# Two key steps' values in one run, and what moves with it, in an attention and expert block on one Trainium2 core

## The chip, the core and the metric

The kernel runs on one core of a Trainium2 chip. The core has a matrix engine (PE, with the loading of its weights shown apart as PEld), a vector engine (DVE), a scalar engine (ACT), a general engine (POOL) and an engine that only issues transfers (SP). Each works through its own queue in order. Matrix products land in PSUM banks, which ACT and DVE read; everything else lies in SBUF. The metric is the device time of one execution in microseconds (us), lower is better.

## The reference, cut to what matters

```
x = layernorm(x + attention(x))        # x: 2 x 1024 x 512, 16 heads of 32
x = layernorm(x + moe(x))              # 8 experts, 256 slots each, and a shared expert

attention: q, k, v = projections of x with low-rank updates
           scores = q k^T / sqrt(32);  attn = softmax(scores);  out = attn v
           out projection with a low-rank update
```

Only the attention's inner part, from scores to `attn v`, is touched by the change. It is full float32 in its result.

## The kernel before, in words

The work is cut into 16 **units** of 128 partitions' worth of heads: two batches, four groups of four heads, two halves of 512 queries. A unit has eight **key steps**, one for each 128 keys, so the main loop (`for t in range(NS)`) has 128 steps, `u, k = t // 8, t % 8`. All five engines' orders are written out by hand there: what the loop issues is what each queue holds, in that order.

A step does this:

- `st_step` (line 620): four PE matmuls, one for each head, scores with keys on the partitions. After each, ACT takes the exponential into one half of a tile `pts[t, 0]` or `pts[t, 1]` (line 629). There are 14 such tiles (`PTB`), seven steps' worth. The four places after the four heads are the step's quarters, and `between[q]` lists what else is issued in quarter q.
- `s1_step` (line 189): one matmul with queries on the partitions, and a DVE maximum over its 512 keys (line 197). Four are done in each step, for a step that comes 12 steps (`LEAD`) later; 32 make the row maxima of one unit. `finish_max` transposes these on PE (line 207) and sends them as two rows into the tile of queries, so that `st_step` subtracts them. It is called from the first `s1_step` of the next unit, at quarter `MPP`.
- `av_step` (line 639): four matmuls of values with the exponentials, each 32 columns wide and in its own column tile of PE, all into one bank `avs[u]`. It is issued for the step before, in the second quarter.
- `adds`: the exponentials of a unit are merged so that their row sums need few matmuls. The table `ADDS` says which: `b` takes a tile as the sum, `d` adds a tile into the next one with a DMA (line 656), `p` and `v` add on POOL or DVE (line 659).
- `finish` (line 672): the row sums, as products with ones, of the merged tile and of the tiles that `direct` names. For most units the sums then go through DRAM to another shape (`sd`, `r16`); `invert` takes the reciprocal there and sends it back (`rd`, then four broadcasts `rb`). From unit `RDIR` on, DVE takes the reciprocal of the whole 128 x 512 tile (line 682).
- `normalize` (lines 711 to 718): DVE multiplies the values with the inverse, ACT copies the high part, DVE subtracts for the low part. For two units DVE does the copy too.
- In steps 65 to 80 four to eight matmuls of the first batch's output projection (`oproj`, line 744) stand at a step's end.

PSUM has three banks for `st_step` (shared with the row sums and the transposed maxima, `one`), three for `s1_step` (`s1p`), two for the values (`avp`).

Loads are issued by SP: keys of a group (two units) into one of two tiles, in halves of 512 keys, the first half at k 6 of the unit before (`K_AT`) and the second at k 0; queries of a unit two units ahead at k 0.

Before the loop come the projections, after it the second half of the output projection, the router and the experts.

Of the kernel before, what the change touches and what calls it, by code (L numbers as in the profile page):

```python
# [13 lines left out]
ALU = mybir.AluOpType  # L14
# [5 lines left out]
B, L, D = 2, 1024, 512  # L20
NU = 16
T = B * L
NH, HD = 16, 32
NG = 4
# [8 lines left out]
LEAD = 12  # L33
LATE, OP_ONE = (0,), 1
NS = NU * 8
# [14 lines left out]
}  # L50
MAN3 = {mybir.EngineType.PE}
MAN4 = MAN2 - MAN3
DIRECT = (7,)
NO_DIR = (NU - 2,)
FIN, FINQ = 4, 1
REC = 5
NRM = 0
K_AT = 6
XTB = 5


ADDS = {
    None: {0: "bb0", 2: "dd1", 3: "pp3", 4: "pp4", 5: "pp2", 6: "pp5", 7: "pp6"},
    NU - 3: {0: "bb0", 2: "dd1", 3: "pp3", 4: "pp4", 5: "pp2", 7: "dd6 pp5"},
    NU - 2: {1: "bb1 dd0", 3: "dd2", 5: "dd4", 6: "vv3", 7: "vv6 vv7 vv5"},
    NU - 1: {1: "bb1 dd0", 3: "dd2", 4: "vv4", 5: "vv5", 6: "vv3 vv6"},
}
OPROJ_AT = (65, 67, 69, 71, 73, 75, 77, 79)
RES_AT = tuple(8 * i + (2 if i % 2 else 6) for i in range(8)) + (70, 74, 86, 90, 100, 102, 106, 110)
RES_ADDS = tuple(t + 3 for t in RES_AT[:14]) + (119, 120)  # L70
RB = 2
# [1 line left out]
AHEAD = 5  # L73
W2_END = {2: (0, 1, 2), 3: (3, 4), 4: (5,)}
W2_AT = {2: (0, 1), 3: (2, 3), 4: (4,), 5: (5,)}
MPJ, MPP = 0, 2
RDIR = NU - 3
FINE, NRME = 2, {NU - 2: 6, NU - 1: 4}
OPROJ1 = 0
NRM_DVE = (NU - 3, NU - 2)  # L80
ROOT_LAG, NORM_LAG = 1, 4
# [17 lines left out]
def kernel(  # L99
# [3 lines left out]
    pe, act, dve, pool, sp = nc.tensor, nc.scalar, nc.vector, nc.gpsimd, nc.sync  # L103

    def f(ap):
        return ap.bitcast(F32)
# [42 lines left out]
    def load_k(g, cs=slice(0, 1024), hs=slice(0, 4)):  # L149
        kt = Ks[g % 2]  # L150
        for blk, hl in ((0, 0), (1, 1), (2, 0)):
            sp.dma_start(
                out=f(kt[32 * blk : 32 * blk + 32, hs, cs]),
                in_=qk_d[1, g // NG, g % NG, hl].rearrange("(h p) t -> p h t", p=32)[:, hs, cs],
            )
# [23 lines left out]
    mts, pts, avs, accs, vts = {}, {}, {}, {}, {}  # L179


    def s1_step(s, part):
        u, j = s // 8, s % 8
        g = u // 2
        if j == 0 and part == 0:
            mts[u] = mp_.tile([P, 16, 2], F32, name=f"mt{u}", tag="mt", bufs=2)
        h, qt, kh = j // 2, 2 * (j % 2) + part // 2, part % 2
        s1 = s1p.tile([P, 512], F32, name=f"s1_{u}_{h}_{qt}_{kh}", tag="s1")
        pe.matmul(  # L189
            s1,  # L190
            Qs[u % 3][0:96, h, qt * P : qt * P + P],
            Ks[g % 2][0:96, h, kh * 512 : kh * 512 + 512],
            start=True,
            stop=True,
        )
        c = h * 4 + qt
        dve.tensor_reduce(mts[u][:, c, kh : kh + 1], s1, AX.X, ALU.max)  # L197
        if j == 7 and part == 3:
            mx = mp_.tile([P, 16], F32, name=f"mx{u}", tag="mx", bufs=2)
            dve.tensor_reduce(mx, mts[u], AX.X, ALU.max)  # L200
            mts[u] = mx
        if j == MPJ and part == MPP and u:
            finish_max(u - 1)

    def finish_max(u):
        mp = one.tile([P, 512], F32, name=f"mp{u}", tag="one")
        pe.transpose(mp[0:16, 0:P], mts[u], ident)
        mh = mp_.tile([16, P], F32R, name=f"mh{u}", tag="mh", bufs=2)
        ml = mp_.tile([16, P], F32R, name=f"ml{u}", tag="ml", bufs=2)
        act.copy(mh, mp[0:16, 0:P])  # L210
        dve.tensor_tensor(ml, mp[0:16, 0:P], f(mh), ALU.subtract)
        for i, m_ in enumerate((mh, ml)):
            sp.dma_start(
                out=f(Qs[u % 3][96 + i : 97 + i, :, :]).rearrange(
                    "o h (q t) -> o (h q) t", t=P
                ),
                in_=f(m_),
            )
# [382 lines left out]
    with ph2, tc.manual_schedule(engines={mybir.EngineType.PE}):  # L601
# [31 lines left out]
        def av_step(t):  # L633
            u, kc = t // 8, t % 8
            g = u // 2
            if kc == 0:
                avs[u] = avp.tile([P, 512], F32, name=f"av{u}", tag="av")
            for h in range(4):
                pe.matmul(  # L639
                    avs[u][32 * h : 32 * h + 32, :],  # L640
                    vts[g][:, kc, 32 * h : 32 * h + 32],
                    pts[t, h // 2][:, h % 2, :],
                    start=kc == 0,
                    stop=kc == 7,
                    skip_group_check=True,
                )

        def adds(t):
            u, kc = t // 8, t % 8
            for op in ADDS.get(u, ADDS[None]).get(kc, "").split():  # L650
                i = u * 8 + int(op[2])
                for pr in range(2):
                    if op[pr] == "b":
                        accs[u, pr] = pts[i, pr]
                    elif op[pr] == "d":
                        pool.dma_start(out=pts[i + 1, pr], in_=pts[i, pr], accum_op=ALU.add)  # L656
                    else:
                        eng = dve if op[pr] == "v" else pool
                        eng.tensor_tensor(accs[u, pr], accs[u, pr], pts[i, pr], ALU.add)  # L659

        def direct(u):
            return () if u in NO_DIR else DIRECT

        fin = {}

# [40 lines left out]
        def normalize(u, parts=(0, 1, 2)):  # L706
            g, qb = u // 2, u % 2
            cs = slice(qb * 512, qb * 512 + 512)
            hi, lo = at_h[:, g % NG, cs], at_l[:, g % NG, cs]
            if 0 in parts:  # L710
                dve.tensor_tensor(avs[u], avs[u], fin[u], ALU.mult)
            if 1 in parts:
                if u in NRM_DVE:
                    dve.tensor_copy(hi, avs[u])
                else:
                    act.copy(hi, avs[u])
            if 2 in parts:
                dve.tensor_tensor(lo, avs[u], f(hi), ALU.subtract)
# [42 lines left out]
        op10 = oproj(1, 0, 3)  # L761
        steps = ExitStack()
        steps.enter_context(tc.manual_schedule(engines=MAN2))
        for t in range(NS):
            u, k = t // 8, t % 8
            if k == 0:

                if u % 2 == 0 and 2 <= u and u // 2 + 1 < B * NG:
                    for hs in (slice(0, 2), slice(2, 4)):
                        load_k(u // 2 + 1, slice(512, 1024), hs)  # L770
                        load_q(u + 2, hs)
                elif u >= 1 and u + 2 < NU:
                    load_q(u + 2)
                if u % 2 and NG <= u // 2 + 1 < B * NG:
                    load_v(u // 2 + 1)

            if k == K_AT and u % 2 and u // 2 + 2 < B * NG:
                load_k(u // 2 + 2, slice(0, 512))
            if t in RES_AT:
                load_res(RES_AT.index(t))  # L780
            between = [[], [], [], []]
            if t + LEAD < NS:
                for q in range(4):
                    between[q].append(lambda q=q: s1_step(t + LEAD, q))
            elif t + LEAD == NS:
                between[0].append(lambda: finish_max(NU - 1))
            if t:
                between[1].append(lambda: av_step(t - 1))
                between[1].append(lambda: adds(t - 1))
                if u and k == (FINE if u == NU - 1 else FIN):  # L790
                    between[1 if u == NU - 1 else FINQ].append(lambda: finish(u - 1))
            if u:
                if k == NRM and 1 < u < NU - 1:
                    for q in range(3):
                        between[q].append(lambda q=q: normalize(u - 2, (q,)))
                if k == NRME.get(u):
                    for q in range(3):
                        between[(0, 3, 3)[q]].append(lambda q=q: normalize(u - 1, (q,)))
            if t in RES_ADDS:
                between[3].append(lambda: add_res(RES_ADDS.index(t)))  # L800
            st_step(t, between)
            if k == REC and 1 <= u <= RDIR:
                invert(u - 1)
            if t in OPROJ_AT:
                op0 = oproj(0, OPROJ_AT.index(t), OPER)
            if OPROJ_AT[0] <= t:
                next(op0, None)
            if t + 1 in OPROJ_AT[1:]:
                run(op0)
            for _, fn in [x for x in later if x[0] == 0]:  # L810
                fn()
            later[:] = [(n - 1, fn) for n, fn in later if n]
            if t - NS >= OPROJ1:
                next(op10, None)
        av_step(NS - 1)
        adds(NS - 1)
        finish(NU - 1)
        normalize(NU - 1, (0,))
# [302 lines left out]
    for st in range(NB):  # L1121
# [18 lines left out]
        if st == NB - 3:  # L1140
            reads_xd(
                sp.dma_start(
                    out=meta, in_=xd_d[:, D : D + 2].rearrange("(j p) c -> p j c", p=P)
# [132 lines left out]
```

## Time and profile before

| | |
|---|---|
| median of 3 runs | 1062.13 us (1060.24 to 1062.37) |
| the profiled execution | 1048.99 us, its span 1047.3 us |
| granted PE clock | 0.996 |
| main loop | about 155 to 606 us |
| experts and the rest after it | about 607 to 1047 us |

The profile is of one execution. A line of its timeline says when an instruction or a row of the same instructions started, how long it took, the engine, the line of the program, the operation, what it wrote and read, how many there are, and in brackets how long the engine was idle before it and what it had waited for. The windows view gives, for each stretch, each engine's busy time and number of instructions.

| stretch, us | PE busy | DVE | ACT | POOL |
|---|---|---|---|---|
| 205.00 to 372.00 | 166.86 | 135.78 | 110.92 | 165.73 |
| 372.00 to 462.00 | 89.49 | 67.51 | 50.19 | 71.75 |
| 462.00 to 560.00 | 98.00 | 80.16 | 67.22 | 96.59 |
| 560.00 to 607.00 | 44.84 | 37.33 | 31.83 | 13.48 |

The first and third are units with all their parts, the second holds most of the output projection's matmuls, the last has the steps for which no `s1_step` is left.

### The profile page before, as it was taken

How to read it: one execution, taken by the hardware profiler on the slowest of the kernel's cores; microseconds unless marked ns; L12 is line 12 of the kernel's file. 1: busy time of each engine (PE TensorE's matmuls, PEld its weight loads, DVE VectorE, ACT ScalarE, POOL GpSimd, SP SyncE). 2: the span in 40 equal slices, each digit the busy share in tenths (PEclk: the TensorE clock that was granted, in tenths of full speed). 3: DMA queues.
4: the chain of work that ended last, by engine and by line, in shares of the span. 5: the costliest groups of instructions: out<-in, count | busy, mean ns of one | idle time of the engine just before them, and what ended most of it. 6: DMA issues, size and time to landing. Idle time of an engine off the chain costs nothing. (4 is left out here: it accounts for less than half of the span.)

```text
span 1047.3 us, 16557 instructions
## 1 busy us (share of the span) xinstructions
PE 1026.7 (98%) x5994; PEld 741.5 (71%) x5994; DVE 687.7 (66%) x1192; ACT 527.2 (50%) x1023; POOL 573.2 (55%) x406
## 2 busy tenths in 40 slices
PE   8999999999999999999999999999999999999995
PEld 6888774444444455545444379899999999999994
DVE  7732788788888878788887974233522567777752
ACT  5422216666666656566666645223222456555552
POOL 4000005999999987879996255000140046676674
PEclk9999999999999999999999999999999999999998
DMA  9876863364646563444657632000182556777721
GB/s 294 278 231 210 250 204 81 87 141 103 141 94 148 120 140 83 100 92 120 150 121 161 142 106 67 22 21 21 41 253 81 156 183 219 253 246 248 256 81 60
DMA packets 86025, 151.93 MB, mean 145 GB/s; under 512 B 15492, under 2 KB 24196, under 8 KB 85944
## 3 DMA queue, kind: packets, MB, share of 16 engines
q1 hardware_dynamic: 76344, 117.31, 37.7%
q0 software_dynamic: 9600, 33.58, 13.6%
q8 instruction: 47, 0.77, 0.3%
q14 instruction: 34, 0.28, 0.1%
HBM read 95.83 MB, written 33.78 MB: 124 GB/s over the span
## 5 line engine op out<-in xcount | busy, mean ns | idle before, releaser
L197 DVE TENSOR_REDUCE mt<-s 128x1 f32<-128x512 f32 x512 | 323.9, 681 | 78.7 <-PE s L189 78.3
L659 POOL TENSOR_TENSOR pt<-pt,pt 128x1024 f32<-128x1024 f32 x138 | 336.0, 2917 | 0.1
L629 ACT ACTIVATE pt<-st 128x512 f32<-128x512 f32 x512 | 269.1, 601 | 131.5 <-PE st L620 114.2
L620 PE MATMUL st<-qs,ks 98*128 98x512 f32 x512 | 213.1, 427 | 1.1 <-DVE x1a L347 0.7
L189 PE MATMUL s<-ks,qs 96*128 96x512 f32 x512 | 200.2, 398 | 1.1 <-DVE mt L197 1.1
L620 PEld LDWEIGHTS st<-qs,ks 98*128 98x128 f32 x512 | 95.6, 188 | 133.0 <-issue 93.1
L656 POOL DMA_DIRECT2D pt<-pt x40 | 36.9, 1101 | 187.2 <-PE st L620 164.2
L890 PE MATMUL h<-xthe,w13s 128*128 128x256 f32 x704 | 129.9, 284 | 0.0
L878 POOL TENSOR_TENSOR w2s<-w2r,w2s 128x512 fp32r<-128x512 f32 x42 | 65.9, 1590 | 93.1 <-ACT w2s L877 92.2
L189 PEld LDWEIGHTS s<-ks,qs 96*128 96x128 f32 x512 | 97.0, 189 | 20.5 <-DVE mt L197 5.8
L890 PEld LDWEIGHTS h<-xthe,w13s 128*128 128x128 f32 x704 | 110.6, 191 | 0.3
L890 PE MATMUL h<-xtle,w13s 128*128 128x256 f32 x352 | 100.2, 285 | 0.1
L639 PE MATMUL av<-pt,vt 128*32 128x512 f32 x512 | 75.3, 605 | 0.0
L1038 POOL DMA_INDIRECT xd_d<-x1a,slot_i x8 | 7.9, 985 | 110.5 <-DVE slot_i L1035 108.4
L639 PE MATMUL av<-pt,x1b 128*32 128x512 f32 x512 | 68.2, 605 | 0.0
L890 PEld LDWEIGHTS h<-xtle,w13s 128*128 128x128 f32 x352 | 67.4, 191 | 1.0 <-DVE xtle L468 0.3
L934 PE MATMUL y<-w2s,hs 128*128 128x512 f32 x260 | 60.9, 390 | 0.0
L934 PEld LDWEIGHTS y<-w2s,hs 128*128 128x128 f32 x260 | 48.2, 188 | 10.2 <-DVE hs L916 0.5
L331 ACT ACTIVATE oh<-o,bqk_sb 128x512 fp32r<-128x512 f32 x32 | 22.0, 690 | 57.1 <-PE o L316 52.7
L901 ACT ACTIVATE sl<-h 128x256 f32<-128x256 f32 x40 | 15.5, 386 | 60.5 <-PE h L890 59.2
L316 PE MATMUL o<-xh,wh 128*128 128x512 f32 x116 | 45.3, 391 | 0.3 <-DVE ol L332 0.3
L316 PE MATMUL o<-xl,wh 128*128 128x512 f32 x116 | 45.3, 390 | 0.1
(830 smaller groups left out, 1831.9 us busy)
## 6 DMA issues: line engine op xcount, KB each, us to landing
pt<-pt POOLq DMA_DIRECT2D x40, 512.0 KB, 6.4
x1a<-in_w_dram SPq DMA_DIRECT2D x24, 512.0 KB, 5.6
w2r<-in_w_dram SPq DMA_DIRECT2D x42, 256.0 KB, 2.9
qkd<-oh SPq DMA_DIRECT2D x32, 256.0 KB, 2.3
qkd<-ol SPq DMA_DIRECT2D x32, 256.0 KB, 2.5
x1b<-in_w_dram SPq DMA_DIRECT2D x16, 512.0 KB, 7.0
qs<-qkd SPq DMA_DIRECT2D x30, 256.0 KB, 4.4
ks<-qkd SPq DMA_DIRECT2D x18, 256.0 KB, 4.6
```

Source lines behind the costliest of these rows:

```text
L189: pe.matmul(s1, Qs[u % 3][0:96, h, qt * P : qt * P + P], Ks[g % 2][0:96, h, kh * 512 : kh * 512 + 512], start=True, stop=True,)
L197: dve.tensor_reduce(mts[u][:, c, kh : kh + 1], s1, AX.X, ALU.max)
L316: pe.matmul(o, lhs, rhs, start=k + i == 0, stop=k + i == KC + 1)
L331: act.activation(oh, o, AF.Identity, bias=bias)
L620: pe.matmul(sb, Ks[g % 2][:, h, kc * P : kc * P + P], Qs[u % 3][:, h, :], start=True, stop=True,)
L629: act.activation(pts[t, h // 2][:, h % 2, :], sb, AF.Exp, scale=SCALE)
L639: pe.matmul(avs[u][32 * h : 32 * h + 32, :], vts[g][:, kc, 32 * h : 32 * h + 32], pts[t, h // 2][:, h % 2, :], start=kc == 0, stop=kc == 7 ...
L656: pool.dma_start(out=pts[i + 1, pr], in_=pts[i, pr], accum_op=ALU.add)
L659: eng.tensor_tensor(accs[u, pr], accs[u, pr], pts[i, pr], ALU.add)
L878: pool.tensor_tensor(hl[:, 1, :], raw, f(hl[:, 0, :]), ALU.subtract)
L890: pe.matmul(hp[:, j * 256 : j * 256 + 256], lhs, rhs[:, k, :], start=n == 0, stop=n == 11,)
L934: pe.matmul(o, lhs, rhs, start=n == 0, stop=n == 16)
```

## The change

- `av_step` is issued for two steps at once, at even steps, in the fourth quarter (`AVQ`).
- The 32 `s1_step` calls of eight steps are no longer one for each quarter. A table `S_AT` gives for each step and quarter how many stand ahead of the values and how many behind them. Their order among themselves is the same. `MPP` goes from 2 to 1.
- `ADDS`: most units now add tile 2 into tile 1 and tile 3 into tile 0 with DMAs, and tiles 4, 5, 6 and 0 into tile 1 on POOL. The DMA's target is now given by the table. Before, one DMA added tile 1 into tile 2, and POOL added tiles 3, 4, 2, 5 and 6 into tile 0.
- `DIRECT`: the last unit takes the row sums of tiles 6 and 7 straight. DVE's adds for it fall from eight to six.
- `FIN`, `REC` and `NRM` give unit offset, step and quarter of the row sums, the inverse and normalize. For most units: row sums at step 4 of the next unit, quarter 1, as before; the inverse at step 6 instead of 5; normalize at step 1 of the unit after, instead of step 0.
- `RDIR` goes up by one: unit 13 takes the way through DRAM.
- Keys are loaded whole at k 0, in two halves of the heads; the load at k 6 is gone.
- The output projection's steps go from 65 to 79 to 66 to 80.

```
-DIRECT = (7,)
-NO_DIR = (NU - 2,)
-FIN, FINQ = 4, 1
-REC = 5
-NRM = 0
-K_AT = 6
+DIRECT = {None: (7,), NU - 2: (), NU - 1: (6, 7)}
+AVQ = 3
+FIN = {None: (1, 4, 1), NU - 3: (1, 3, 1), NU - 2: (1, 2, 3)}
+REC = {None: (1, 6, 3), NU - 3: (1, 5, 3)}
+NRM = {
+    None: ((2, 1, 0), (2, 1, 2), (2, 1, 2)),
+    NU - 3: ((2, 0, 1), (2, 0, 1), (2, 0, 1)),
+    NU - 2: ((1, 4, 1), (1, 4, 1), (1, 4, 1)),
+}
+S_AT = (
+    ((0, 0), (0, 1), (1, 0), (1, 0)), ((0, 0), (0, 1), (1, 1), (0, 0)),
+    ((0, 2), (1, 0), (0, 0), (0, 2)), ((0, 0), (0, 1), (0, 2), (0, 0)),
+    ((0, 1), (1, 2), (0, 1), (1, 1)), ((1, 0), (0, 0), (2, 0), (1, 0)),
+    ((0, 0), (1, 0), (0, 1), (1, 0)), ((0, 1), (1, 0), (0, 0), (2, 0)),
+)
 ADDS = {
-    None: {0: "bb0", 2: "dd1", 3: "pp3", 4: "pp4", 5: "pp2", 6: "pp5", 7: "pp6"},
-    NU - 3: {0: "bb0", 2: "dd1", 3: "pp3", 4: "pp4", 5: "pp2", 7: "dd6 pp5"},
-    NU - 2: {1: "bb1 dd0", 3: "dd2", 5: "dd4", 6: "vv3", 7: "vv6 vv7 vv5"},
-    NU - 1: {1: "bb1 dd0", 3: "dd2", 4: "vv4", 5: "vv5", 6: "vv3 vv6"},
+    None: {1: "bb1 dd21", 2: "dd30", 3: "pp4", 4: "pp5", 5: "pp6", 6: "pp0"},
+    NU - 2: {1: "bb1 dd01", 3: "dd23", 5: "dd45 vv6 vv3", 6: "vv7", 7: "vv5"},
+    NU - 1: {1: "bb1 dd01", 3: "dd23 vv4", 4: "vv5", 6: "vv3"},
 }
-OPROJ_AT = (65, 67, 69, 71, 73, 75, 77, 79)
+OPROJ_AT = (66, 68, 70, 72, 74, 76, 78, 80)
-MPJ, MPP = 0, 2
-RDIR = NU - 3
-FINE, NRME = 2, {NU - 2: 6, NU - 1: 4}
+MPJ, MPP = 0, 1
+RDIR = NU - 2
...
-                        pool.dma_start(out=pts[i + 1, pr], in_=pts[i, pr], accum_op=ALU.add)
+                        to = u * 8 + int(op[3])
+                        pool.dma_start(out=pts[to, pr], in_=pts[i, pr], accum_op=ALU.add)
...
+        quarters = iter([(s_, q) for s_ in range(LEAD, NS) for q in range(4)])
+        def maxima():
+            for s_, q in quarters:
+                s1_step(s_, q)
+                return
+        def at_step(table, t, q):
+            for v in range(max(t // 8 - 2, 0), t // 8):
+                at = table.get(v, table[None])
+                at = at[q] if isinstance(at[0], tuple) else at
+                if (v + at[0]) * 8 + at[1] == t:
+                    yield v
...
-                        load_k(u // 2 + 1, slice(512, 1024), hs)
+                        load_k(u // 2 + 1, hs=hs)
                         load_q(u + 2, hs)
...
-            if k == K_AT and u % 2 and u // 2 + 2 < B * NG:
-                load_k(u // 2 + 2, slice(0, 512))
...
+            for q in range(4):
+                between[q] += [maxima] * S_AT[k][q][0]
+            if t + LEAD == NS:
+                between[AVQ].append(lambda: finish_max(NU - 1))
+            if t and t % 2 == 0:
+                between[AVQ].append(lambda: (av_step(t - 2), av_step(t - 1)))
+            for v in at_step(FIN, t, 0):
+                between[FIN.get(v, FIN[None])[2]].append(lambda v=v: finish(v))
+            for q in range(4):
+                between[q] += [maxima] * S_AT[k][q][1]
             if t:
+                between[AVQ].append(lambda: adds(t - 1))
+            for q in range(3):
+                for v in at_step(NRM, t, q):
+                    between[NRM.get(v, NRM[None])[q][2]].append(lambda v=v, q=q: normalize(v, (q,)))
+            for v in at_step(REC, t, 0):
+                if v < RDIR:
+                    between[REC.get(v, REC[None])[2]].append(lambda v=v: invert(v))
...
+        av_step(NS - 2)
         av_step(NS - 1)
```

More of the change, by code (lines that the diff above doesn't have):

```diff
@@ L661, in direct @@
         def direct(u):
-            return () if u in NO_DIR else DIRECT
+            return DIRECT.get(u, DIRECT[None])
         fin = {}
@@ L781 @@
             between = [[], [], [], []]
[L782 to L786, printed above, removed]
-            if t:
[L788 to L798, printed above, removed]
+            for q in range(4):
[8 more added lines that the diff above has]
+                between[q] += [maxima] * S_AT[k][q][1]
+            if t:
+                between[AVQ].append(lambda: adds(t - 1))
[5 more added lines that the diff above has]
+                    between[REC.get(v, REC[None])[2]].append(lambda v=v: invert(v))
             if t in RES_ADDS:
@@ L801 @@
             st_step(t, between)
-            if k == REC and 1 <= u <= RDIR:
-                invert(u - 1)
             if t in OPROJ_AT:
```

## The prediction

> I call a score matmul of line 620 a T, one of line 189 an s, a run of value matmuls (line 639) an A, a run of row sums (line 672) an F. A unit is eight key steps, k0 to k7.
>
> **What bounds the kernel now.** The chain that ended last starts at 1030.73 us and says nothing of attention. I read the page's first part, then the windows view of one steady unit (columns: PE, PEld, DVE, ACT, POOL, clock, DMA share, GB/s).
>
> ```profile
> PE 1026.7 (98%) x5994; PEld 741.5 (71%) x5994; DVE 687.7 (66%) x1192; ACT 527.2 (50%) x1023; POOL 573.2 (55%) x406
> ...
> 231.65:258.30 26.65, 26.65 (x146) 13.13 (x146) 21.54 (x38) 17.71 (x35) 26.65 (x15) 1.00 0.46 101
> ```
>
> A unit lasts 26.65 us, and neither PE nor POOL is ever idle. Which sets the pace is seen in PE's timeline. Starts count, since ends are modelled.
>
> ```profile
> 258.03 0.50 PE L620 MATMUL st<-qs,ks 98*128 98x512 f32 x1
> 258.37 0.39 PE L189 MATMUL s<-ks,qs 96*128 96x512 f32 x1
> 258.60 0.39 PE L620 MATMUL st<-qs,ks 98*128 98x512 f32 x1
> ...
> 259.77 0.39 PE L189 MATMUL s<-ks,qs 96*128 96x512 f32 x1
> 260.10 1.07 PE L639 MATMUL av<-pt,x1b 128*32 128x512 f32 x8
> 261.09 0.50 PE L620 MATMUL st<-qs,ks 98*128 98x512 f32 x1
> ...
> 276.36 1.90 PE L672 MATMUL sm<-pt,ones 128*32 128x512 f32 x16
> ```
>
> T and s start every 0.235. An A starts 0.33 after the s before it, the next T 0.99 later, and its successor after 0.34: an A adds 0.33 + 0.99 + 0.34 - 2 x 0.235 = 1.19. Its eight records are two passes over four column tiles. F's four passes give (1.90 - 0.59 - 0.02)/3 = 0.43 for each further pass. PE's unit is 64 x 0.235 + 7 A x 1.19 + one A joined to F, 1.19 + 4 x 0.43 = 2.91, + 0.3 for the transposed maxima: 26.6 of the measured 26.65. PE's own work is the bound; POOL is just as full, but PE does not wait for it.
>
> **Values of two steps in one run.** A joined run has four passes: 1.19 + 2 x 0.43 = 2.05 instead of 2.38. But F moves to k4's second quarter, away from the A in the fourth, and costs 2.05 alone instead of 1.72. A unit: 7 x 1.19 + 2.91 = 11.24 before, 4 x 2.05 + 2.05 = 10.25 after; gain 1.0.
>
> A rule speaks against this. The Trainium skill, TensorE: Matmul & The Clock Gate, Part 3 ("What overlaps and what doesn't"), lets a weight load overlap a running matmul only where its row group differs. The value tiles use the same 128 rows, so each further pass would pay its load too (0.11 at line 639): a pair would save 0.33 - 0.22 = 0.11, and a unit about 0.1. The row decides otherwise:
>
> ```profile
> 260.09 0.16 PEld L639 LDWEIGHTS av<-pt,x1b 128*32 128x32 f32 x8 [0.36 <-issue]
> ```
>
> All eight loads end 0.16 after the run begins, the second pass's under the first pass. I take 0.43.
>
> **The new order of T and s.** They now come in bursts between two A's, and ACT, DVE and three PSUM banks for each kind must keep up.
>
> ```profile
> 258.63 2.07 ACT L629 ACTIVATE pt<-st 128x512 f32<-128x512 f32 x4 [1.07 <-PE st L620]
> ...
> 264.39 0.59 ACT L716 CAST at_h<-av 128x512 fp32r<-128x512 f32 x1 [0.67 <-DVE av L711]
> ```
> ```profile
> 258.80 2.48 DVE L197 TENSOR_REDUCE mt<-s 128x1 f32<-128x512 f32 x4 [0.48 <-PE s L189]
> ...
> 205.14 0.50 PE L189 MATMUL s<-ks,qs 96*128 96x512 f32 x1 [0.47 <-DVE mt L197]
> ```
>
> In a row an exponential takes (2.07 - 0.60)/3 = 0.49, a maximum (2.48 - 0.68)/3 = 0.60. The last line shows what full banks do: PE waits for the reduce. I walk each stretch by hand from its first T. In k1 and k2 PE's order is T, T s, T s s, T, T s s, T s, T, T, A. Exponentials 0 to 2 start at 0.55, 1.05, 1.5; normalize's copy (line 716), moved here from k0, follows at 2.0; exponential 3 at 2.5, exponential 4 from 3.0 to 3.6. The eighth T reuses that bank and starts at 3.65 instead of 3.15: 0.5 lost. DVE, with two normalize operations of 0.69 here, holds the fifth s by 0.1 in the same time. From k2's end to F the fifth s waits 0.1 to 0.2, in k6 the last one 0.1, in k7 and k0 none. With 0.1 for each weight load that a stall uncovers, 0.9 a unit. A steady unit then takes 26.65 - 1.0 + 0.9 = 26.55: nearly all is given back. Behind a late normalize stands the A of k2, which reuses its bank: the subtraction ends 3.5 after that first T, the A starts at 4.1. Exponential tiles live a step longer: at k4 all seven steps' buffers are taken (k0 to k4, and 1 and 7 of the unit before), which fits once POOL has freed tile 0, some 2 us ahead. Bounds: no stall, 25.65; twice the stall, 27.45. I take the walk, since the 205.14 row shows such waits.
>
> The gain stays where PE has other work: in units 8 and 9 output matmuls (2.8 a pair) let ACT and DVE catch up, 1.0 each. Units 0 and 1 have no normalize: 1.2 together. The ten other full units: 0.1 each, 1.0. Unit 14's first half: two pairs less F alone and stalls, a loss of 0.3. Sum: 2.0 + 1.2 + 1.0 - 0.3 = 3.9.
>
> **The last 12 steps** have no s.
>
> ```profile
> 566.52 1.07 PE L639 MATMUL av<-pt,vt 128*32 128x512 f32 x8
> ...
> 570.36 1.64 PE L639 MATMUL av<-pt,vt 128*32 128x512 f32 x8
> ...
> 573.05 1.65 PE L639 MATMUL av<-pt,vt 128*32 128x512 f32 x8
> ...
> 586.49 2.19 PE L672 MATMUL sm<-pt,ones 128*32 128x512 f32 x8 [1.09 <-DVE pt L659]
> ...
> 606.37 0.50 PE L744 MATMUL op<-wo_h,at_h 128*128 128x512 f32 x1
> ```
>
> A step lasts 2.69, since its A waits for exponentials of the step just before. From 566.52 to 606.37 is 39.85; without unit 13's F (1.7, counted above), 38.1. After, an A finds its exponentials done; the eighth T waits for a bank until 2.2, and A takes 2.2, so a pair lasts 4.36. Six pairs: 26.2. Unit 14's F adds 0.9, and waits: eight DVE merges of 1.14, three normalize steps and the third DMA merge's landing leave it 2.7 late. From the last A to the projection 5.65 (3.75 before: the A holds two steps, F one direct step more). 35.4 in all; gain 2.7.
>
> **Merges.** POOL's adds fall from 138 to 112, its DMA merges rise from 40 to 66.
>
> ```profile
> 268.29 5.41 POOL L659 TENSOR_TENSOR pt<-pt,pt 128x1024 f32<-128x1024 f32 x2
> 274.03 1.77 POOL L656 DMA_DIRECT2D pt<-pt  x2 [0.32 <-PE st L620]
> ```
> ```profile
> DMA to landing us min/median/max: 4.4/6.4/10.8
> ```
>
> An add takes 5.41 - 3.07 = 2.34 in a row (3.07 is one alone), a DMA issue 0.57. A unit of POOL: 10 x 2.34 + 2 x 0.57 = 24.5 before, 8 x 2.34 + 4 x 0.57 = 21.0 after, plus residual adds of 1.05. Worth nothing on PE, which did not wait. But the first add of k4 now waits for a DMA of k2 to land; behind it stand seven adds, and the next unit's F behind those. The first of two DMAs lands after 4.45 in most units (the second after 6.4), the latest after 10.8 beside weight loads. The page DMA: Bandwidth & Descriptors (the SWDGE fit) would give 3.2; I use 4.45. POOL's circle is 4.5 + 18.7 + 1.05 = 24.3, under 26.55: hidden.
>
> **Moved at no cost.** Keys whole at k0: three DMAs of 256 KB leave k6, six of 128 KB become six of 256. With SP's 0.43 per issue and 5.4 to land, the first six are there 9 to 13 us after k7 ends; the first s that reads them stands after F in k4, 15 us after. Late, they would hold PE one for one. The inverse's five DMAs are queued on SP ahead of these loads, issued 3 us after k6's DVE reciprocal, which stands behind k6's reduces; they land at k1's start, as normalize needs them; cover gone, DVE waits and s behind it. Unit 13's reciprocal (3.36) becomes seven DMAs and one of 0.25, in slack.
>
> **Sum.** 3.9 + 2.7 = 6.6 off the profiled 1048.99 (span 1047.3): 1042.4. The median of the runs is 13.1 higher, and nothing shows where; I take the same 6.6 off 1062.1: 1055.5. The three runs spread 2.1 us, 0.2%, about what tells from no change.
>
> **Rivals.** The covers hold: no burst stalls, so all units keep 1.0. 1.3 + 13.0 + 0.3 + 2.7 = 17.3, 1044.8. For it: DVE's and ACT's sums (21.5 and 17.7 a unit) fit; against it, three banks and the copy in k1.
>
> Slower: the landing. POOL's circle passes PE's 26.55 once a merge takes over 6.8 to land on average. Key and query loads (2.3 MB) run until about k2's end in every second unit. At 8 us, between 4.45 and 10.8, a unit takes 27.75: 1.2 x 12 units - 3 of slack before F = 11.4 more, 1066.9.
>
> No change: the stalls are 1.4 a unit instead of 0.9, 0.5 x 13 = 6.5 back: 1062.
>
> **Chances.** Forecast 0.45, covers hold 0.25, landing 0.18, no change 0.12. The forecast's own range is 1050 to 1060; 0.42 of its 0.45 is faster, 0.03 same. With the covers' 0.25: faster 0.67. Same: 0.03 + 0.08 = 0.11. Slower: 0.18 + 0.04 = 0.22. Half of the covers' case ends near 1046, half of the landing's above 1067: 1046 to 1067.
>
> **What would show it.** Right: A's of 16 records starting 0.33 after their predecessor, the T after them about 1.85 later; the eighth T of k1 and k2 waiting for ACT; a unit of 26.5; A's 4.4 apart at the end. Wrong: T or s waiting for POOL or a DMA, adds idle until pt has landed, units under 26 or over 27.

## The result

| kernel | chip where the kernel before takes | median, us (runs) | before beside it, us (runs) | ratio, 95% interval |
|---|---|---|---|---|
| after | 1061 | 1062.80 (12) | 1060.74 (12) | 1.0016 [1.0006, 1.0026] |
| after, again (after_again) | 1062 | 1063.84 (22) | 1062.15 (62) | 1.0014 [1.0005, 1.0022] |
| after, again (after_b) | 1050 | 1051.18 (22) | 1050.23 (27) | 1.0011 [1.0004, 1.0018] |

The change costs 0.1 to 0.2%, 1 to 2 us, where 6.6 us of gain were forecast. None of the three intervals holds 1, so the loss is small but clear of the noise. The forecast of 1055.5 missed it, in sign too. That 1062.8 falls on the number of the "no change" rival (1062) is luck: as the traces show, it is not for that rival's reason.

Chips differ by more than the kernels: before takes about 1050 us on some and 1061 to 1062 on others. So the two traces are compared stage by stage, and the changed kernel twice: its first profile (span 1059.7 us) and one from a chip like that of the profile of before (span 1048.1 us). First that first profile: the page's first part, then the windows view of a steady unit, of units 8 to 10 and of the end of attention (columns as in the prediction). The line after it is of the kernel before, units 8 to 10.

```profile
PE 1029.5 (97%) x6002; PEld 745.6 (70%) x6002; DVE 678.6 (64%) x1190; ACT 526.4 (50%) x1024; POOL 535.4 (51%) x406
```
```profile
233.60:260.10 26.50, 26.50 (x147) 13.19 (x145) 21.40 (x39) 17.59 (x37) 24.58 (x15) 1.00 0.62 131
...
366.50:474.30 107.80, 104.69 (x532) 57.64 (x531) 78.78 (x145) 61.08 (x114) 76.78 (x55) 1.00 0.61 131
...
554.70:609.76 55.06, 49.79 (x275) 20.25 (x273) 37.15 (x45) 37.87 (x73) 20.97 (x17) 0.94 0.59 126
```
```profile
368.80:472.50 103.70, 103.19 (x532) 56.96 (x531) 78.69 (x144) 60.77 (x114) 85.45 (x55) 1.00 0.46 103
```

The steady unit is 26.50 (26.65 before): the forecast said 26.55. POOL is no longer full. Units 8 to 10 are 107.8 long (103.7 before), with PE idle for 3.1 of it (0.5 before), and in the last stretch PE's granted clock falls to 0.94 on average. The following ledger adds up the stages, each from the first T of a unit (T, s, A and F as in the prediction):

| stage | before | after, chip of 1050 | difference | forecast |
|---|---|---|---|---|
| units 0 and 1 | 53.15 | 51.21 | -1.9 | -1.2 |
| units 2 to 7 | 160.00 | 159.22 | -0.8 | -0.6 |
| units 8 to 10 | 103.70 | 107.86 | **+4.2** | **-2.1** |
| units 11 to 13 | 79.90 | 80.30 | +0.4 | -0.3 |
| units 14 and 15, to the projection | 53.97 | 54.73 | **+0.8** | **-2.4** |
| from there to the last matmul | 429.1 | 429.1 | 0 | 0 |
| last matmul to the end | 11.79 | 9.87 | -1.9 | 0 |

With 0.2 before the loop, the rows make the 0.8 us between the spans 1047.3 and 1048.1. In the first profile the rows of attention are the same within 0.4; only the expert stage is longer there, by 11.

**The steady unit** behaves as worked out. PE's weight loads for a joined run, in the first profile of the changed kernel:

```profile
241.35 0.16 PEld L651 LDWEIGHTS av<-pt,x1b 128*32 128x32 f32 x8 [0.25 <-DVE mt L209]
241.80 0.13 PEld L651 LDWEIGHTS av<-pt,x1b 128*32 128x32 f32 x4 [0.30 <-issue]
242.23 0.13 PEld L651 LDWEIGHTS av<-pt,x1b 128*32 128x32 f32 x4 [0.30 <-issue]
```

The run starts at 241.35; the third and fourth passes' loads lie at 241.80 and 242.23, under running passes. The 15 starts inside a run take 1.33 us, the way out 0.52. With the usual 0.33 on the way in (this run came 0.1 later) that is 0.33 + 1.33 + 0.52 + 0.34 - 0.47 = 2.05, the forecast's price. About half of what was given back stands in k1 and k2, where normalize now stands. Its first operation on DVE, and PE's last two T ahead of the run above:

```profile
237.47 0.70 DVE L724 TENSOR_TENSOR av<-av,rb 128x512 f32<-128x512 f32 x1 [0.86 <-DMA rb<-rd]
```
```profile
240.50 0.91 PE L632 MATMUL st<-qs,ks 98*128 98x512 f32 x2
```

The two start 0.41 apart instead of 0.235. The second, the eighth T of k1 and k2, starts 3.70 after the first (walked: 3.65), and the A 4.13 after it (walked: 4.1). The walk put the loss of 0.5 into that one T; in the trace four starts are 0.1 to 0.18 late. I call a start of a T or s late by what it comes after the one before beyond 0.235. Added up over a unit, late starts amount to 0.03 us before and 1.0 after (forecast: 0.9).

**POOL** in the changed kernel, around the landings of a unit:

```profile
222.59 2.38 POOL L672 TENSOR_TENSOR pt<-pt,pt 128x1024 f32<-128x1024 f32 x1 [1.51 <-DMA pt<-pt]
226.38 9.46 POOL L672 TENSOR_TENSOR pt<-pt,pt 128x1024 f32<-128x1024 f32 x4 [1.41 <-DMA pt<-pt]
```

POOL waits for merges to land, as forecast (1.5 and 1.4 us here). PE's waits in units 2 to 7 name neither POOL nor a DMA, so it doesn't feel it.

**The end of attention**, where the A's answer those at 566.52, 570.36 and 573.05 of before (PE's timeline, first profile of the changed kernel):

```profile
576.40 1.92 PE L651 MATMUL av<-pt,vt 128*32 128x512 f32 x16
...
580.90 1.92 PE L651 MATMUL av<-pt,vt 128*32 128x512 f32 x16
...
587.98 0.80 PE L632 MATMUL st<-qs,ks 98*128 98x512 f32 x1 [2.27 <-ACT pt L641]
589.14 3.64 PE L651 MATMUL av<-pt,vt 128*32 128x512 f32 x16 [0.36 <-DVE at_l L731]
592.56 1.57 PE L685 MATMUL sm<-pt,ones 128*32 128x512 f32 x8
```

Pairs are 4.50 apart. Then a T waits 2.27 and an A 0.36 more, and this A takes 3.64 instead of 1.92: from 586.8 to 593.6 the granted clock is half. The T waits for ACT, and ACT for a merge to land in the tile that it is to write:

```profile
587.33 3.04 ACT L641 ACTIVATE pt<-st 128x512 f32<-128x512 f32 x6 [1.91 <-DMA pt<-pt]
```

### The profile page after: what moved, and what is told of

Same layout as the page of the kernel before. It is cut to its first block, busy times and chain, and to the rows that moved or that the text cites. A ratio compares the mean times of both kernels' runs of the same rounds, so it can differ in the third digit from the quotient of the medians.

```text
span 1059.7 us, 16542 instructions
## 1 busy us (share of the span) xinstructions
PE 1029.5 (97%) x6002; PEld 745.6 (70%) x6002; DVE 678.6 (64%) x1190; ACT 526.4 (50%) x1024; POOL 535.4 (51%) x406
## 5 line engine op out<-in xcount | busy, mean ns | idle before, releaser
L209 DVE TENSOR_REDUCE mt<-s 128x1 f32<-128x512 f32 x512 | 318.6, 681 | 79.4 <-PE s L201 79.2
L672 POOL TENSOR_TENSOR pt<-pt,pt 128x1024 f32<-128x1024 f32 x112 | 264.2, 2384 | 33.3 <-ACT pt L641 18.0
L632 PE MATMUL st<-qs,ks 98*128 98x512 f32 x512 | 192.0, 421 | 8.1 <-ACT pt L641 6.2
L201 PE MATMUL s<-ks,qs 96*128 96x512 f32 x512 | 195.3, 415 | 1.6 <-DVE mt L209 1.1
L669 POOL DMA_DIRECT2D pt<-pt x66 | 58.0, 999 | 199.5 <-PE s L201 168.5
L201 PEld LDWEIGHTS s<-ks,qs 96*128 96x128 f32 x512 | 94.2, 188 | 71.4 <-DVE mt L209 45.8
L651 PE MATMUL av<-pt,vt 128*32 128x512 f32 x512 | 64.0, 613 | 0.4 <-DVE at_l L731 0.4
L651 PE MATMUL av<-pt,x1b 128*32 128x512 f32 x512 | 61.6, 598 | 0.0
```

The source lines that it names most:

```text
L201: pe.matmul(s1, Qs[u % 3][0:96, h, qt * P : qt * P + P], Ks[g % 2][0:96, h, kh * 512 : kh * 512 + 512], start=True, stop=True,)
L632: pe.matmul(sb, Ks[g % 2][:, h, kc * P : kc * P + P], Qs[u % 3][:, h, :], start=True, stop=True,)
L651: pe.matmul(avs[u][32 * h : 32 * h + 32, :], vts[g][:, kc, 32 * h : 32 * h + 32], pts[t, h // 2][:, h % 2, :], start=kc == 0, stop=kc == 7 ...
L669: pool.dma_start(out=pts[to, pr], in_=pts[i, pr], accum_op=ALU.add)
```

## The experiments

All changes are made to the changed kernel. First what the chips do, then the two stages that went wrong, then the two steps that went right.

### The chip under the forecast

Unchanged kernel before, three times (before_again, before_chip, before_chip2).

> The kernel before, profiled once more. The profile that the prediction was made from lasted 1049, its timed runs 1061 to 1062. Theory: attention takes the same time again (first score matmul 155.7, projection after the loop at 606.4 us), and the 12 us more of other executions lie in the expert stage, as a wait of PE for nothing that the profile shows, followed by half a clock, as the changed kernel has it at 770 to 785 us. Rival: the 12 us are spread over attention too, so units last longer than 26.65.

> The kernel before, profiled beside the runs below. Theory: what parts its profiled 1049 us from the 1061 us of its other runs is not in attention but in the expert stage, from about 755 to 780 us, where the matmuls come in ones and twos while POOL scatters the tokens; on a chip where the runs take about 1061 us this profile shows it too, some 9 to 12 us, with units as before. Rival: that stretch is the changed kernel's own; then the profile shows none of it.

> The kernel before, profiled once more. Theory: on a chip where it takes about 1061 us, the expert stage shows the stall between 755 and 790 us (9 to 12 us, matmuls in ones and twos, no clear wait), on a chip where it takes about 1049 us it shows none; units as before in either case. Rival: on a chip of 1061 us the time is lost elsewhere in this kernel.

Measured: 1049.05, 1050.15 and 1048.06 us, all on chips where before has a median of 1049 to 1050, and none with the stall. All five profiles of changed kernels from chips where before takes 1061 to 1062 show it; here the first one, beside a kernel before from a chip of 1050 (windows view):

```profile
760.00:790.00 30.00, 23.35 (x130) 19.41 (x130) 5.68 (x12) 4.13 (x11) 14.42 (x15) 0.83 0.83 241
```
```profile
760.00:790.00 30.00, 30.00 (x218) 28.48 (x217) 8.81 (x20) 7.03 (x19) 11.10 (x12) 1.00 0.82 254
```

In the first, PE does 130 matmuls where the other does 218, while POOL scatters the tokens; the trace names no semaphore for it. From the projection to the last matmul these five take 440.0 to 442.9 us, 11 to 14 more than the 428.8 to 429.2 of all profiles from the chips of 1050, the changed kernel's among them. So for changed kernels it follows the chip. That before has it too on such a chip fits its longer runs there, but no profile shows it: none of the three came to lie on one. It stays open, and so does its cause.

### Units 8 to 10: where the output projection stands

The first guess was the third score bank, which the projection's accumulator holds over a step.

```
-OPER = 4
+OPER = 12
```

> The changed kernel, with a projection's 12 matmuls in one go at the even step's end instead of 4 and 8 over two steps. Theory: over two steps its accumulator holds one of the three banks of the score matmuls, so that bursts of those find two; done at once it gives the bank back before the burst, and units 8 to 10 take 103.5 us or less instead of 107.8: 4 us faster than the change, 2 us faster than before. Rival: the residual's normalization on ACT and DVE makes the waits there: no more than 1 us.

Measured: 1056.6 us, 1.0067 [1.0054, 1.0081] of before; units 8 to 10 took 115.1 instead of 107.8. The guess was wrong in direction: the bank is held for less time, and the stage is longer. What PE waits for in units 8 to 10 (view of waits: engine, line, what it waited for, us in total, times, longest), in the kernel before, the changed one and this one:

```profile
PE st L620 <- ACT pt L629: 0.4, 2, 0.2
```
```profile
PE st L632 <- ACT pt L641: 2.0, 8, 0.3
PE st L632 <- DVE x1a L762: 0.5, 1, 0.5
PE s L201 <- DVE mt L209: 0.2, 1, 0.2
```
```profile
PE s L201 <- DVE mt L209: 5.3, 8, 1.2
```

The waits moved from T to s: all twelve output matmuls now stand behind the A. In the even step PE has one long stretch of other matmuls, a cover under which ACT and DVE can catch up, and in the odd step none. This gave the second theory: it counts where the output matmuls stand relative to the A. They were moved to the odd steps, which have no A.

```
-OPER = 4
+OPER = 12
-OPROJ_AT = (66, 68, 70, 72, 74, 76, 78, 80)
+OPROJ_AT = (67, 69, 71, 73, 75, 77, 79, 81)
```

> Output projection of the first batch at odd steps' ends (67 to 81) and its twelve matmuls in one go, everything else as changed. Theory: in the changed kernel the value run and the first output matmuls stand at the same place (an even step's end), so nothing covers the odd steps, and an output accumulator holds one of the three score banks through the odd step; parted from the value run, ACT and DVE catch up twice in a pair of steps: units 8 to 10 take 103 to 104 together (107.8 as changed), 4 us faster than the changed kernel. Rival: DVE's work for the output (some 2.5 us a pair) is itself too much for bursts: the waits stay or move to the max matmuls, as with twelve in one go at the even steps (115): 107 or more, no gain.

Measured: 1059.47 us where before took 1062.15: 0.9972 [0.9960, 0.9984], and 4.4 us under the changed kernel beside it (1063.84). Units 8 to 10: 103.7, as the theory had it. PE waits there for exponentials only twice; one wait of 0.5 for the output's addition remains beside it:

```profile
PE st L632 <- ACT pt L641: 0.6, 2, 0.4
```

The same place with the old split (`OPROJ_AT` alone) was to part place from split.

> Output projection of the first batch at the odd steps' ends (67 to 81), four and then eight matmuls as in the changed kernel. Theory: it is the place that counts: 4 matmuls at an odd step's end and 8 behind the value run leave the score matmuls without a third bank only in the step that ends with a value run; units 8 to 10 take 104 to 105 (103.7 with twelve in one go, 107.8 as changed), 3 to 4 us faster than the changed kernel. Rival: the split is what counts, since the accumulator still holds a score bank for a step: 106.5 to 108, no gain.

Measured: 1056.04 us, 1.0061 [1.0047, 1.0075] of before, units 8 to 10 in 112.9. Neither theory had it: the odd start alone makes it worse than the changed kernel. Seen by what stands where, the four kernels are one series, though. With the split and the odd start, eight of twelve matmuls fall into the even step, behind the A:

| of twelve, at the odd step's end | 0 (op12) | 4 (op_odd4) | 8 (changed) | 12 (op_odd) |
|---|---|---|---|---|
| units 8 to 10, us | 115.1 | 112.9 | 107.9 | 103.7 |
| late starts of T and s in them, us | 13.1 | 13.1 | 8.7 | 4.6 |

Before, late starts there were 0.5. The first two differ in time but not in late starts; op12 alone has a half clock in this stage, for 6.8 us. From there on both fall as matmuls leave the A's step. My reading: ACT and DVE use a stretch of other matmuls only up to what they are behind; two covers at one place are worth one, and the burst after them is twice as long.

Two other things move with the place, though. DVE's addition of the output and its statistics (1.7 us) follow the last of the twelve: in op12 and op_odd4 they fall into the odd step, in the other two into the even one. In op_odd4 they hold up the maxima:

```profile
442.37 0.69 DVE L762 TENSOR_TENSOR x1a<-op,x1a 128x512 f32<-128x512 f32 x1 [2.95 <-PE op L757]
```
```profile
444.92 0.50 PE L201 MATMUL s<-ks,qs 96*128 96x512 f32 x1 [0.83 <-DVE mt L209]
```

And with the split the output's bank is held over a step, in op_odd4 and the changed kernel, but not in the others. At equal split the place alone makes 11.4 us (op12 to op_odd) and 5.0 (op_odd4 to changed), so the place is shown to count. How much of that is the cover, and how much DVE's work that moves along, was not parted.

### The last steps of attention

The merge of tile 4 into tile 5 was the first suspect (unit 14; DVE adds instead), alone and with op12.

```
-    NU - 2: {1: "bb1 dd01", 3: "dd23", 5: "dd45 vv6 vv3", 6: "vv7", 7: "vv5"},
+    NU - 2: {1: "bb1 dd01", 3: "dd23", 4: "vv4", 5: "vv5 vv6 vv3", 6: "vv7"},
```

> The changed kernel, unit 14 with tile 4 added on DVE instead of a third DMA merge. Theory: at 583 to 588 us ACT waits for that merge to land before it can write the tile again, PE waits 2.3 us for ACT, and falls to half its clock for 6.8 us: without the merge the wait and the half clock go, 5 us faster than the change. Rival: DVE's two more adds (2.3) are on the path to unit 14's row sums, or another merge holds the tile: no more than 1 us.

> Both edits together. Theory: they are apart in time, so the gains add: 9 us faster than the change, 7 faster than before. Rival: one of them is not the cause; the sum of what the two show alone.

Measured: 1054.35 us, 1.0050 [1.0036, 1.0063] of before, and 1061.29, 1.0109 [1.0093, 1.0124]; the half clock stays (588.3 to 595.1 us in the first). The trace of tail_dve gives the reason: with no DMA to wait for, the A of steps 120 and 121 now waits 4.2 us for unit 13's value bank, which normalize frees, and normalize stands behind eight merges on DVE. So it was put ahead of the last four.

```
-    NU - 3: ((2, 0, 1), (2, 0, 1), (2, 0, 1)),
+    NU - 3: ((1, 7, 1), (1, 7, 1), (1, 7, 1)),
-    NU - 2: {1: "bb1 dd01", 3: "dd23", 5: "dd45 vv6 vv3", 6: "vv7", 7: "vv5"},
+    NU - 2: {1: "bb1 dd01", 3: "dd23", 4: "vv4", 5: "vv5 vv6", 6: "vv7 vv3"},
```

> The changed kernel beside the kernel before on one chip, as the base of the other runs. Theory: it is about 3.4 us slower (units 8 to 10 lose 4.1, the end of attention 1.9 and unit 14's and 15's steps some 2, against 4 to 5 gained in units 0 to 7 and 11 to 14): 1052.7 where before takes 1049.3. Rival: the expert stage, which took 9 us more in the changed kernel's profile, belongs to the change; then 1058 and more.

> Unit 13's normalize is put ahead of the last of unit 14's merges (step 119 instead of 120), and unit 14's tiles 4 and 5 are merged on DVE instead of by a DMA. Theory: the value run of steps 120 and 121 waits for the value bank of unit 13, which normalize frees, and normalize stands behind eight merges on DVE; in front of them it frees the bank about 582 to 583 us, the run starts at its own time of 585.4 instead of 589.1, and without the wait of 2.3 to 3 us PE's clock is not halved (2.4 more): 4 to 6 us faster than the changed kernel. Rival: the row sums of unit 14 are what is late (the merges' end, near 587 in any order): then the wait moves to the row sums, and the clock still falls: within 1.5 us of the changed kernel.

> Both edits at once. Theory: they add up, 8 to 10 us faster than the changed kernel, about 4 to 6 faster than before. Rival: one of them is only a moved wait, so no more than 5 us faster than the changed kernel.

Measured: changed 1063.84 (1.0014 of before: 1.7 us slower, where 3.4 was expected), tail_order 1064.14, 1.0021 [1.0014, 1.0029]; with op_odd's edit (two_fixes) 1060.15, 0.9980 [0.9973, 0.9987]. So the total is the rival's, within 1.5 us of the changed kernel, and together with op_odd's edit the gain is 3.7 instead of 8 to 10. But the trace of tail_order shows the gain in its place:

```profile
586.11 1.92 PE L651 MATMUL av<-pt,vt 128*32 128x512 f32 x16 [0.58 <-DVE at_l L731]
589.51 2.19 PE L685 MATMUL sm<-pt,ones 128*32 128x512 f32 x8 [1.48 <-DVE pt L672]
```

The A is at 586.11 instead of 589.14 and F waits only 1.5 for DVE, the clock stays full, and the stretch from unit 15's first T to the projection takes 27.9 us (30.4 in the changed kernel). This gain is lost again at the very end. From the start of the last matmul to the end:

| kernels | transfers on POOL's queue besides the gathers and scatters | us |
|---|---|---|
| before; adds_old | 40; 38 | 11.79; 11.69 |
| changed, op12, op_odd, op_odd4, rec5, single | 66 | 9.86 to 9.87 |
| tail_order, two_fixes | 64 | 13.45 |

The two edits of tail_dve (64) and both (64) made the stage behind attention 3.6 longer in the same way. To test it, tail_order got two transfers more on POOL's queue.

```
+        pad_d = dram.tile([P, D], F32, name="pad_d")
...
+            if t == 100:
+                for _ in range(2):
+                    pool.dma_start(out=pad_d, in_=bo_bc)
```

> The reordered tail of unit 14, and two transfers of 256 KB more on POOL's queue at step 100, so that this queue has as many transfers as in the changed kernel; they carry nothing that is used. Theory: the reordering saves 4 to 5 us in attention, and all kernels with two transfers less showed a drain of POOL at the very end that is 3.6 us longer (13.45 us from the last matmul to the end instead of 9.87); with the number restored it is 9.87 again, and the kernel is 3 to 5 us faster than the changed kernel. Rival: the longer drain comes from something else in that edit: 13.45 stays, within 1 us of the changed kernel.

Measured: 1055.37 us, 1.0057 [1.0043, 1.0070] of before. The last lines of POOL, in tail_order (span 1061.3 us) and in tail_pad (1053.1):

```profile
1052.36 1.05 POOL L1127 DMA_INDIRECT out_dram<-be,meta  x1 [1.13 <-ACT be L609]
```
```profile
1048.41 1.05 POOL L1131 DMA_INDIRECT out_dram<-be,meta  x1 [1.72 <-ACT be L609]
```

From the last scatter's issue to the end it is 8.9 us and 4.7 us. From the last matmul on it is 9.82 in tail_pad, 3.6 less than in tail_order: the two transfers shorten the drain, as the theory had it. The total is worse all the same, since in this edit both transfers go to one place, and the second waits for the first, on POOL.

```profile
526.19 0.57 POOL L797 DMA_DIRECT2D pad_d<-bo_bc  x1 [10.96 <-DMA pad_d<-bo_bc]
```

POOL stood for 11 us, and 17 us after that a T waited 3.8 us for an exponential that had no tile: unit 13 took 34.9 instead of 27.2, with 6.8 us at half clock in it. ACT, which writes these tiles, had by then waited 5.9 us for POOL. So POOL's lead there is about 5 us, an estimate from these two (11 less 5.9).

### Together

op_odd, tail_order, and the two transfers to two places at steps 2 and 3.

```
+        pads = [dram.tile([P, D], F32, name=f"pad{n}") for n in range(2)]
...
+            if t in (2, 3):
+                pool.dma_start(out=pads[t - 2], in_=bo_bc)
```

> Twelve output matmuls at the odd steps' ends, the reordered tail of unit 14, and two transfers on POOL's queue (256 KB each, not used by anything) at steps 2 and 3, to two places, so that neither waits for the other. Theory: the three parts add up: units 8 to 10 in 103.7 (107.8), the end of attention 2.6 to 4.8 sooner, POOL's last drain as short as in the changed kernel (9.87 from the last matmul to the end): 7 to 9 us faster than the changed kernel and about 4 to 6 faster than the kernel before. Rival: the drain is not a matter of that number and is 13.45 again: 3 to 5 us faster than the changed kernel.

> The changed kernel again, as the base of these runs. Theory: 1.5 to 4 us slower than the kernel before on any chip (a ratio of 1.0014 to 1.004). Rival: where the expert stage shows no stall, the change gains, and it is faster than before.

> The kernel with the three edits again. Theory: all it gains is in attention and at the last drain, so it is 4 to 7 us faster than the kernel before on any chip. Rival: on a chip with the stall in the expert stage the stall eats the gain: less than 2 us.

Measured: best2 1044.45 us, 0.9943 [0.9928, 0.9958] of before, beside after_b with 1051.18 (1.0011): 6.7 us under the changed kernel (7 to 9 expected) and 5.8 under before. On one more chip of 1050, best2_b 1044.65, 0.9952 [0.9939, 0.9966]. The drain is 9.8 again and units 8 to 10 take 103.7 in both, and best2_b has the full clock through all of attention. What is left is unit 13, at 29.1 in best2 and 27.4 in best2_b. So it is faster than both kernels on chips of 1050. On a chip of 1061 it was not run.

### The inverse

Added to op_odd:

```
-REC = {None: (1, 6, 3), NU - 3: (1, 5, 3)}
+REC = {None: (1, 5, 3), NU - 3: (1, 5, 3)}
```

> Twelve output matmuls at the odd steps' ends, and the inverse sent at step 5 instead of step 6. Theory: the inverse sent over a unit's end lands late in some units (normalize began 1.7 to 2.3 us late at 291 and 532 us, with max matmuls of 1 to 1.7 us waiting behind it); a step earlier it is always there: units 5 and 13 take 26.5 to 26.6 (26.9 and 27.3 to 29.1), 1 to 3 us faster than with the output projection's edit alone, 5 to 7 faster than the changed kernel. Rival: the inverse's input isn't there at step 5, and DVE waits for it with the max matmuls behind: no gain, or units over 26.6.

Measured: 1049.18 us, 0.9996 [0.9989, 1.0003] of before, where op_odd had 0.9972 on another chip. Both theories have a half of it. In the changed kernel (after_again) normalize is late in units 5 and 13; with the earlier inverse, in rec5, the wait sits at the reciprocal. DVE's timeline of the one and the other:

```profile
533.35 0.70 DVE L724 TENSOR_TENSOR av<-av,rb 128x512 f32<-128x512 f32 x1 [2.31 <-DMA rb<-rd]
```
```profile
204.43 0.25 DVE L709 RECIPROCAL r<-r 128x16 f32<-128x16 f32 x1 [1.99 <-DMA r<-sd]
```

Units 5 and 13 fall to 26.5 and 26.6 (27.3 and 27.4 in op_odd), while units 1, 2, 6 and 7 rise to 26.9 to 27.6 (26.3 to 26.5). From the first T to the projection rec5 takes 453.2 us and op_odd 451.8: step 6 is the better of the two.

### The two steps that held

```
-            if t and t % 2 == 0:
-                between[AVQ].append(lambda: (av_step(t - 2), av_step(t - 1)))
+            if t:
+                between[AVQ].append(lambda: av_step(t - 1))
...
-        av_step(NS - 2)
         av_step(NS - 1)
```

> Only the joined run undone: the values of one step in every step's fourth quarter, everything else as changed. Theory: a unit's matmuls cost 1.32 more (four more entries at 0.33), but each step now has a value run in which ACT and DVE catch up, so of the 0.9 us of waits most go: units 2 to 7 at 26.6 to 27.0, and units 8 to 10, where no step is without cover any more, at 103 to 105 instead of 107.8: within 3 us of the changed kernel. Rival: the waits come from normalize and the order of the maxima, not from the joined run; then they stay, units of 27.5 and more, over 10 us slower than the changed kernel.

Measured: 1090.24 us, 1.0372 [1.0351, 1.0394] of before, and 39 us over the changed kernel, where at most 3 were expected. A unit takes 28.69 where nothing more disturbs it, and its one wait is new:

```profile
PE av L651 <- DVE at_l L731: 1.6, 1, 1.6
```

The first A of a unit now stands in k1, where normalize has not freed the bank; 28.69 less this 1.6 is 27.1, about the price expected, and late starts of T and s fall to 0.35 a unit. So in a steady unit the waits of T and s do come from the bursts between joined runs, and the joined run also makes room for normalize in k1. The expectation for the total was far off, since that new wait was not seen: there are eight stretches of 3.4 us and more at half clock in attention. Units 8 to 10 take 119.9 instead of 103 to 105, and their late starts stay at 8.0 (8.7 as changed) though every step now has an A. It stands at the step's end, next to the output matmuls, in the odd steps too; in the kernel before it stood in the second quarter. So in this stage the waits do not come from joining the values of two steps; they fit a cover that lies beside another one.

```
-    None: {1: "bb1 dd21", 2: "dd30", 3: "pp4", 4: "pp5", 5: "pp6", 6: "pp0"},
+    None: {0: "bb0", 2: "dd12", 3: "pp3", 4: "pp4", 5: "pp2", 6: "pp5", 7: "pp6"},
```

> Only the merges of the steady units as before (one DMA merge, POOL adds of five tiles into tile 0), everything else as changed. Theory: POOL's 25.5 us a unit still fit into PE's 26.5, so PE doesn't notice: units 2 to 7 at 26.5 to 26.6, the whole within 1.5 us of the changed kernel, apart from the last drain, which follows the number of transfers (26 less). Rival: POOL is now late with the row sums or with freeing tiles, and score matmuls wait for it: units of 26.8 and more, over 4 us slower than the changed kernel.

In this kernel tile 1 is added into tile 2 before the values of tile 2 are taken, so step 2's values are weighted with tile 1's exponentials too, and the result is another sum than attention: its time alone is of use. Measured: 1064.14 us, 1.0146 [1.0126, 1.0166] of before, and 13 us over the changed kernel, where at most 1.5 were expected apart from the drain. Units are 26.5 where that merge has landed in time, and 28 to 28.5 in most others:

```profile
225.86 1.05 PE L651 MATMUL av<-pt,x1b 128*32 128x512 f32 x4
227.36 1.91 PE L651 MATMUL av<-pt,x1b 128*32 128x512 f32 x12 [0.46 <-DMA pt<-pt]
```

The A of steps 2 and 3 is broken off until the merge has landed. What POOL's longer work alone would cost it does not tell, but at 26.53 and 26.52 (units 3 and 5) it cost nothing. It shows why the change has to merge into tiles that the values have read.

## Why the prediction was wrong

**Right, within 0.3 us.** The bound (PE, not POOL); the joined run's 2.05; a gain of 1.0 a unit in matmuls; 0.9 of it given back (1.0 measured); the steady unit at 26.55 (26.50 to 26.55); loads under running passes (0.45 and 0.88 us after the run's start, in passes of 0.43), where the trace differs from the rule of the Trainium skill, TensorE: Matmul & The Clock Gate, Part 3, "What overlaps and what doesn't"; merges worth nothing to PE; keys in time (no s waits for a DMA). Units 0 and 1 gained 1.9 instead of 1.2.

**The step that failed: "in units 8 and 9 output matmuls (2.8 a pair) let ACT and DVE catch up, 1.0 each."** It let these two units keep the whole gain of 1.0, as if the output matmuls covered every stall, without walking the stage. They were no such cover: in the changed kernel, four of twelve stand right behind the A, the odd step's eight come only after the burst, and DVE has the output's addition and statistics to do (1.7 us each time), which the step put at nothing. Late starts went from 0.5 to 8.7 us in units 8 to 10, and the stage lost 4.2 instead of gaining 2.1: 6.3 of the 7.4 us between forecast (-6.6) and the 0.8 of the ledger. That the place of the output matmuls makes the loss the series of four kernels shows, and op_odd brings the stage back to the 103.7 of before, though not to the forecast gain: 4.6 us of late starts remain. Which part of the loss is the cover and which DVE's work stays open.

**The last 12 steps: forecast -2.7 and +0.3, measured +0.8.** The wait has the forecast's size (2.7 late; 2.27 + 0.36 in the first profile), but not its path, so the match is in part luck: it falls on a T, through the tile that a merge holds, and then on the A, through the value bank, and not on F. Not seen were the half clock behind it (in the first profile the A takes 1.7 and F 0.5 longer) and pairs of 4.45 to 4.50 instead of 4.36 (six of them, up to 0.8): up to 3.0 of the 3.5 by which that profile's 55.06 passes the forecast.

**Moved at no cost** was nearly so: the inverse does land late in some units; in the changed kernel's three profiles that goes with 0 to 0.7 us in unit 5 and 0.6 to 2.6 in unit 13, the 2.6 with a half clock in it.

**Not in the forecast:** 1.9 us less in POOL's last drain. Without it the change would be 2.8 us slower than before on this ledger.

**The rivals.** "The covers hold" failed already in the steady units, where the stalls came. The landing did hold POOL, but not PE. "No change" has the right number from larger stalls in all units; the stalls were as forecast in the steady ones, and sat in units 8 to 10. The 13.1 us that "nothing shows" go with the chip; where before loses them is open.

## What to carry to other kernels

In this kernel, work of another kind in PE's queue helped ACT and DVE only where it did not stand beside other such work: when one cover is moved or joined, look where the others stand, and walk the stage with the extra work by itself, with its own DVE work. A wait that is sized right still has to be followed to the clock and to the next queue. And where a gain is seen in the trace at its place but not in the total, compare every later stage too, down to the drain at the end.

## What the hardware did unexpectedly

- **The last drain.** From the last matmul to the end: 11.7 to 11.8 us with 38 and 40 transfers on POOL's queue besides the 48 gathers and scatters, 13.45 with 64, 9.8 to 9.9 with 66, whether 66 came from merges or from two transfers without use; 64 and 66 were seen so on both kinds of chip. Whether the number, the packets or something else that changes with them counts was not parted.
- **Half clock after short waits.** Waits of 2.3 us (a T, the first profile) and 3.3 us (a T, after_b) went with 6.8 and 3.4 us at half clock, and in after_again two s that started 1.1 and 0.4 late with 3.4 us; waits of 0.6 and 1.5 in tail_order with none. The runs give no length from which on it falls.
- **Chips.** The kernel before takes 1049 to 1050 us on four chips and 1062 on another. In the changed kernels profiled where it takes 1061 to 1062, the difference is 11 to 14 us of the expert stage, around 760 to 790 us.
